# Head 0 of a two-layer graph attention network: raw products first, the logarithm later, some logits earlier

## The chip, the cores and the metric

The kernel runs on one NeuronCore of a Trainium2 chip. The metric is the device time of one execution in microseconds. Three runs of the kernel before are given (median 628.09), and one more execution was profiled. Engines: PE multiplies matrices, DVE and ACT work on vectors, POOL and SP here mainly issue transfers. Each engine works through its own queue in order; engines wait for each other by semaphores.

## The reference

A graph of 512 nodes with 16,896 edges (8,192 random pairs in both directions, and a loop at each node). Node features have 768 columns. Two graph attention layers are followed by a residual and a layer norm; the first layer has 8 heads of 768 columns, the second has one.

```python
h = (x @ W).reshape(n, H, C)
alpha_s = einsum('nhc,hc->nh', h, a_s);  alpha_d = einsum('nhc,hc->nh', h, a_d)
e = leaky_relu(alpha_s[src] + alpha_d[dst], 0.2)
e = exp(e - segment_max(e, dst)[dst])
alpha = e / (segment_sum(e, dst)[dst] + 1e-16)
out = segment_sum(h[src] * alpha[:, :, None], dst) + b
# layer 1 (8 heads, concatenated) -> elu -> layer 2 (1 head)
# result: layernorm(x + layer 2)
```

## The kernel before

Everything is float32. The edges become a dense 512 x 512 matrix of counts `cnt` (how often an edge occurs) and a mask `absent` (a huge number where there is none), in four tiles of 128 target nodes. They are made by products of one-hot matrices while the first projection runs.

Per head of layer 1 there are four stages: the *projection* `HS[h] = x W1[h]`; the *softmax*, for each tile `lift` (ACT), `leak` and `rank` (DVE), an exponential (ACT), `weigh` (DVE), then a transposition by DMA (`turn_out` on ACT and SP, `turn_in` on ACT) into the transposed weights `PT`; the *aggregation* of the features with `PT`, with bias and ELU, into `gT`; and the *second product* `gT W2[h]`, added to `h2`. The softmax of head h+1 runs beside the second product of head h, and its logits (`half_logits`, line 417: a row sum of features times `a_s` or `a_d`, eight for each head, two for each tile) beside the aggregation of head h.

Matrix products use schemes that spare multiplications. The aggregation splits its operands into halves and makes, for each of three chunks `c` of 128 feature columns, seven products P1 to P7 of two matmuls each (each shows as two records) with 256 columns. P1 and P2 multiply raw blocks of the features and of the near half of `PT`. P6, P5, P3 and P4, P7 need sums on one side at least: `left_sums` (lines 932 to 935) of the features, `right_sums` (943 to 946) of `PT`, made by DVE. The results of the seven products are combined by DVE in `u`, `w` and `zr`, and ACT applies the ELU. A product that is added to a bank of another one (P2 to P1, P4 to P7, P3 to P5) has to wait until that bank's first content was read.

The aggregation of heads 0 to 6 is `mixed` (line 949): for each chunk P1, P6, P7, P2, P5, P4, P3. That of head 7 is `last_mixed` (line 1001): the right sums are issued first, then PE does P1 of chunks 0 and 1 and P2 of chunks 0 and 1, and then the other products chunk by chunk. PSUM has five banks named `mm` for all of this, taken in turn.

The second product of head 0 is `by_halves` (line 432): P1, P2, P6, P7, P4, P5, P3, each for two row blocks of three chunk steps. P1 and P2 are emptied by ACT (L445, L446), the others by DVE (L447 to L451). The sums of `gT` are L389 to L392, those of the weights L401 and L402.

In head 0 the softmax multiplies by the counts. From head 1 on the counts are folded into the mask: `logarithm` (line 656) turns `cnt` into its logarithm on ACT, and `fold_count` (line 660) makes `absent - log(cnt)` on DVE. Before the change the logarithm of tile 0 is taken at the end of the projection of head 1, that of tiles 1 to 3 behind the first product of the aggregation of head 0. ACT loads another table for a logarithm (ACT_TABLE_LOAD), and again for the next exponential.

The order of all instructions on each engine is written out by hand; the program is issued in that order (`tc.manual_schedule()`). Near the change: lines 1102 to 1117 issue the second half of head 1's projection with the softmax of head 0 beside it; line 1191 the aggregation of head 0, with lists of what DVE does between its steps; lines 1196 to 1240 the second product of head 0 with the softmax of head 1 beside it. On SP, line 1194 reloads `a_s` and `a_d` for head 2, and `attended` (line 1143) loads four pieces for the second layer, both behind `row_out` (line 622), which sends the source logits of head 1 through DRAM and back as a row.

Of the kernel before, what the change touches and what calls it, by code (L numbers as in the profile page):

```python
# [20 lines left out]
NO_EDGE = -1e30  # L21
# [16 lines left out]
def gat_pass(  # L38
# [515 lines left out]
    def counted(t, ps):  # L554

        nc.scalar.copy(cnt[:, t, :], ps[:, :N])
        nc.scalar.activation(absent[:, t, :], ps[:, :N], AF.Relu, bias=far, scale=NO_EDGE)

    def counted_by_steps(t, ps):


        steps = ohp.tile([P, N + 1], F32, name="steps")
        nc.scalar.activation(steps[:, 1:], ps[:, :N], AF.Copy, scale=0.5)
        nc.scalar.activation(steps[:, :1], ps[:, N - 1:N], AF.Copy, scale=-0.5)
        nc.vector.tensor_tensor(cnt[:, t, :], steps[:, 1:], steps[:, :N], op=ALU.subtract)
        nc.scalar.activation(absent[:, t, :], cnt[:, t, :], AF.Relu, bias=far, scale=NO_EDGE)

    def first_projection(h, XA, B_, between):

# [86 lines left out]
    def logarithm(tiles):  # L656
        nc.scalar.activation(cnt[:, tiles, :], cnt[:, tiles, :], AF.Ln, bias=tiny)
        folded.append(True)
# [19 lines left out]
    if not general:  # L678
# [95 lines left out]
        for n, batch in enumerate(batches):  # L774
            for k in sorted({c // quarter for c in batch} - made):
                destinations(k)
                made.add(k)
            if n + 1 < len(batches):
                sources(kinds(batch, False), waiting)
            if n + 2 == len(batches):  # L780
                sources(kinds(batches[-1], False), [])
            ahead = kinds(batches[n + 1], True) if n + 1 < len(batches) else []
            items_here = max(wants[n] - pos if n < len(wants) else 0, 1)
            share = len(ahead) // (items_here + 1) if n == 0 else -(-len(ahead) // items_here)
            waiting = []
            for f in extra.pop(n, []):
                f()
            while n < len(wants) and pos < wants[n]:
                if pos == wholes:
                    pairs = projection(1, XA, B1)  # L790
                    items += [(m, e, False) for m, e in pairs[:4]]
                multiply, empty, on_vector = items[pos]
                multiply()
                if on_vector:
                    waiting.append(empty)
                else:
                    empty()
                pos += 1
                for t, r in turns.get(pos, []):
                    turn_x(t, r)  # L800
                if pos == 1:
                    nc.scalar.activation(nidx, idx, AF.Copy, bias=0.5, scale=-1.0)
                part = 0 if n == 0 and pos == 2 else share
                for c in ahead[:part]:
                    one_hot(c, True)
                del ahead[:part]
            for c in ahead:
                one_hot(c, True)
            if n == 2:
                turn_b1()  # L810
            if n + 1 == len(batches):
                spread(0)
                q = [lift(0, t) for t in range(NT)]
                for t in range(NT - 1):
                    leak(q[t])
                for t in range(NT - 1):
                    rank(q[t], t)
            if n == 0:
                pst = mm.tile([P, 512], F32, name="mm")
                nc.tensor.matmul(pst[:1, :1], found, ones, start=True, stop=True)  # L820
            if n == 3:
                again = nc.values_load(flag[:1, :1], min_val=0, max_val=E)
            count(batch, n + 1 == len(batches))
# [125 lines left out]
    def mixed(h, A_, B_, fill, ends=()):  # L949

        tt = nc.vector.tensor_tensor
        behind = []

        def some(c, j):
            for f in fill[c][j]:
                f()

        for c in range(HK):
            u = work.tile([P, HN], F32, name="u")
            w = work.tile([P, HN], F32, name="w")  # L960
            zr = work.tile([P, N], F32, name="zr", bufs=3)
            bank = {}

            def part(p, over=None):
                if over is None:
                    bank[p] = mm.tile([P, 512], F32, name="mm")
                else:
                    bank[p] = bank[over]
                for k in range(2):
                    nc.tensor.matmul(bank[p][:, :HN], A_[p][:, k, c * P:(c + 1) * P], B_[p][:, k, :],  # L970
                                     start=over is None and k == 0, stop=k == 1, skip_group_check=True)
                return bank[p][:, :HN]

            nc.scalar.copy(u, part("P1"))  # L974
            if h == c == 0:
                logarithm(slice(1, NT))
            if behind:

                behind = behind[0]()
            tt(u, u, part("P6"), op=ALU.add)  # L980
            tt(w, u, part("P7"), op=ALU.add)
            for f in behind[:1]:
                f()
            near_l = elu(h, c, part("P2", over="P1"), near, "l")
            some(c, 0)
            tt(zr[:, far_], part("P5"), w, op=ALU.subtract)
            for f in behind[1:] + list(ends[:1]) * (c == HK - 1):
                f()
            tt(zr[:, near], u, part("P4", over="P7"), op=ALU.add)
            near_l()  # L990
            for f in list(ends[1:]) * (c == HK - 1):
                f()
            tt(u, part("P3", over="P5"), u, op=ALU.subtract)
            some(c, 1)

            def others(c=c, u=u, zr=zr):
                return [elu(h, HK + c, zr, slice(0, N), "r", spare=zr), elu(h, c, u, far_, "l", spare=u)]
            behind = [others]
        return behind[0]()

    def last_mixed(A_, B_, sums, fill):

        h, tt = H - 1, nc.vector.tensor_tensor
        banks, us, nears = {}, {}, {}

        def part(c, p, over=None):
# [87 lines left out]

    AA, lsums = left_sums(0)
    BB, rsums = right_sums()
    some_logits = half_logits(1, 2)

    def give(t):
        turn_out(q[t], t, weigh(q[t], t, scale=False))  # L1100
# [2 lines left out]
    beside = {4: [lambda: give(0)], 5: [done[4]], 6: [done[5]], 7: [done[6], lambda: give(1)],  # L1103
              8: [done[7], lambda: leak(q[3]), lambda: rank(q[3], 3), lambda: turn_in(0)], 9: [lambda: give(2), done[8]],
              10: [lambda: give(3), lambda: turn_in(1), done[9]], 11: [done[10], lsums[0]],
              12: [done[11], lambda: turn_in(2), *lsums[1:3]], 13: [done[12], lambda: turn_in(3), lambda: logarithm(slice(0, 1)), *rsums[:2]]}
    for n in range(4, 14):
        pairs[n][0]()
        for f in beside[n]:
# [2 lines left out]
            load_w2(0, "w1")()  # L1112
            B2, pending = right(W2[0], "w1")
    pairs[13][1]()
    for f in rsums[2:]:
        f()
    besides = [lsums[3], *some_logits]

    def g_thirds(h):

# [40 lines left out]
    def score(t):  # L1161
        q[t] = lift(h + 1, t)
# [11 lines left out]
    for h in range(H - 1):  # L1174
# [4 lines left out]
        elif h:  # L1179
# [3 lines left out]
                nc.sync.dma_start(v, row_bcast(a))  # L1183
                A[H].append(v)
            last_sum = load_w2(H - 1, "w2")
        halves = [half_logits(h + 1, t) for t in ((0, 1) if h else (0, 1, 3))]
        sources, targets = zip(*halves)
        row = [lambda: row_out(h + 1)]
        if h == 0:
            GA, gsums = left(gT, gS)  # L1190
            finish = mixed(0, AA, BB, [[[besides[0], sources[1]], [besides[1], sources[0]]], [[], [sources[2]] + row + besides[2:]],
                                       [[], list(targets)]])
            load_w1(2)()
            load_a(2, a_src1[2], a_dst1[2])
            attend = attended(0)
# [8 lines left out]
            gsums[1]()  # L1204
            pending[0]()
            pairs[2][0]()
            gsums[2]()
            pairs[3][0]()
            gsums[3]()
            pending[1]()  # L1210
            pairs[2][1]()
            pairs[3][1]()
            fold_count(0)
            score(0)
            for n in range(2, 7):
                (m0, e0), (m1, e1) = pairs[2 * n:2 * n + 2]
                m0()
                m1()
                if n == 3:
                    e0()  # L1220
                if n < 6:
                    scored(n - 2)
                if n < 5:
                    score(n - 1)
                if n == 6:
                    turn_in(0)
                    out_by_dma(2)
                if n != 3:
                    e0()
                if 3 < n < 6:  # L1230
                    out_by_dma(n - 4)
                if n == 6:
                    out_by_dma(3)
                    B2, sums2, load_pairs, load_first, load_rest = load_second(1)
                    load_pairs()
                    load_first()
                    load_rest()
                e1()
                if n < 5:
                    fold_count(n - 1)  # L1240
# [156 lines left out]

    first, second_, third_, fourth = (given(t) for t in range(NT))
    BB, rsums = right_sums()
    finish = last_mixed(AA, BB, [*rsums, lsums[3], lambda: nc.vector.memset(rows, 0.0)], {(1, 1): second_[:1], (2, 1): first})  # L1400
    every = slice(0, N)
    pairs = second(GA, B2)

# [131 lines left out]
```

## Time and profile before

| | |
|---|---|
| runs | 627.80, 628.09, 628.95 us; median 628.09 |
| profiled execution | 628.25 us; its span 626.5 us; granted PE clock 0.997 |
| PE busy | 615.7 us, 98% of the span |
| DVE, ACT, POOL busy | 528.8, 339.2, 148.9 us |
| second half of head 1's projection ends | at 79.0 us |
| aggregation of head 0 | 79.0 to 99.2 us |
| second product of head 0 | 99.2 to 126.4 us |
| aggregation of head 7 | 549.0 to 567.2 us |

In a timeline a row gives start and duration in microseconds, the engine, the line of the kernel, the operation, output and inputs, the shape and how many instructions were merged; in brackets is the engine's idle time before it and what ended it. PEld is the loading of weights into PE, which runs ahead of the matmuls. "q" behind an engine is its queue, which issues transfers. In a list of waits: engine and line, what was waited for, microseconds in total, times, the longest.

### The profile page before, as it was taken

Reading aid. Unit: us, or ns where it says so; the run is one execution under the profiler, and the core shown is the slowest. Engines: PE = TensorE matmul, PEld = TensorE weight load, DVE = VectorE, ACT = ScalarE, POOL = GpSimd, SP = SyncE. Lnnn points to the kernel's source line nnn. Section 1 sums busy time; section 2 is a strip of 40 time slices with the busy share of each in tenths; the row PEclk is TensorE's granted clock in tenths of the full one; section 3 lists DMA queues with packets and bytes.
Section 4 is the critical chain, followed back from the end, with each engine's and each line's share of the span. In section 5 each row is a group of like instructions: output and inputs, shape, how many; then the busy total and the mean of one; then the engine's idle time right before and its main releaser. Section 6 shows DMA issues by size and latency. Waiting matters only on the chain.

```text
span 626.5 us, 8547 instructions
## 1 busy us (share of the span) xinstructions
PE 615.7 (98%) x2765; PEld 483.6 (77%) x2765; DVE 528.8 (84%) x1125; ACT 339.2 (54%) x602; POOL 148.9 (24%) x177
## 2 busy tenths in 40 slices
PE   8999999999999999999999999999999999999995
PEld 5555576556888888888888888888888888886553
DVE  8988979888899879978799778977898778978785
ACT  5874876650658236651658246751658146754361
POOL 1300011013333234323342323323342313010000
PEclk9999999999999999999999999999999999999998
DMA  8994297789999999999999998999999995590042
GB/s 298 326 235 110 67 265 238 188 216 267 249 222 142 326 256 198 172 274 219 248 237 175 308 250 194 194 283 226 228 215 192 317 280 91 107 261 17 17 76 79
DMA packets 109568, 129.45 MB, mean 207 GB/s; under 512 B 41622, under 2 KB 90446, under 8 KB 108750
## 3 DMA queue, kind: packets, MB, share of 16 engines
q1 hardware_dynamic: 75518, 91.35, 47.3%
q0 software_dynamic: 33568, 36.90, 38.4%
q10 hardware_dynamic: 432, 0.59, 0.3%
q8 instruction: 24, 0.39, 0.3%
q14 instruction: 26, 0.21, 0.1%
HBM read 99.84 MB, written 2.90 MB: 164 GB/s over the span
## 4 chain that ended last, share of the span: by engine, by line
PE 86%; ACT 1%; DMA 1%; DVE 1%; issue 0%
PE mm L480 46%; PE mm L970 20%; PE mm L409 13%; PE mm L1481 3%; PE mm L1012 3%; DMA zr<-pS 0%; DMA zr<-nr 0%; ACT PT L907 0%; ACT pS L902 0%; ACT q L899 0%; PE tr L1390 0%; ACT nr L902 0%; PE tr L891 0%; PE bc L1425 0%; DVE hs L1485 0%; PE tr L1427 0%
## 5 line engine op out<-in xcount | busy, mean ns | idle before, releaser
L486 ACT ACTIVATE hs<-mm 128x512 f32<-128x512 f32 x30 | 17.9, 596 | 86.1 <-PE mm L480 85.8
L970 PE MATMUL mm<-PT,hs 128*128 128x256 f32 x252 | 61.3, 379 | 0.0
L970 PEld LDWEIGHTS mm<-PT,hs 128*128 128x128 f32 x252 | 47.8, 190 | 7.3 <-ACT u L974 0.4
L649 ACT ACTIVATE q<-q,nmax 128x512 f32<-128x512 f32 x32 | 23.1, 721 | 51.2 <-DVE nmax L645 50.8
L493 DVE TENSOR_TENSOR hs<-hs,mm 128x512 f32<-128x512 f32 x45 | 30.9, 686 | 22.1 <-PE mm L480 21.3
L491 POOL DMA_DIRECT2D h<-pass x22 | 26.5, 1319 | 80.9 <-ACT pass L490 80.9
L970 PE MATMUL mm<-pS,gS 128*128 128x256 f32 x168 | 43.2, 380 | 1.3 <-DVE pS L944 1.3
L493 DVE TENSOR_TENSOR h<-h,mm 128x512 f32<-128x512 f32 x56 | 38.3, 684 | 6.3 <-PE mm L480 5.8
L907 ACT COPY PT<-zr 128x1024 uint16<-128x1024 uint16 x34 | 39.3, 1155 | 4.2 <-DMA zr<-pS 3.6
L480 PE MATMUL mm<-w2r,xT 128*128 128x256 f32 x160 | 37.8, 379 | 0.0
L480 PE MATMUL mm<-w2r,gT 128*128 128x256 f32 x160 | 37.0, 379 | 0.0
L970 PEld LDWEIGHTS mm<-pS,gS 128*128 128x128 f32 x168 | 31.8, 190 | 5.9 <-DVE pS L944 1.7
L133 POOL DMA_DIRECT2D w1t<-in_L_gnn_W_dram x18 | 29.2, 1642 | 30.4 <-PE mm L409 26.9
L480 PE MATMUL mm<-w1t,hs 128*128 128x256 f32 x144 | 34.1, 380 | 0.0
L480 PE MATMUL mm<-w1r,hs 128*128 128x256 f32 x144 | 34.1, 379 | 0.0
L480 PE MATMUL mm<-w1r,gS 128*128 128x256 f32 x144 | 34.0, 379 | 0.0
L480 PEld LDWEIGHTS mm<-w2r,gT 128*128 128x128 f32 x160 | 30.4, 190 | 4.1
L480 PEld LDWEIGHTS mm<-w2r,xT 128*128 128x128 f32 x160 | 30.4, 190 | 4.1
L974 ACT COPY u<-mm 128x256 f32<-128x256 f32 x21 | 7.8, 371 | 45.5 <-PE mm L970 45.5
L716 DVE TENSOR_SCALAR os<-nodes,idx 128x512 bf16<-128x512 f16 x104 | 29.3, 354 | 1.4 <-PE tr L742 1.4
L480 PEld LDWEIGHTS mm<-w1t,hs 128*128 128x128 f32 x144 | 27.3, 190 | 3.9 <-ACT absent L490 0.2
L480 PEld LDWEIGHTS mm<-w1r,hs 128*128 128x128 f32 x144 | 27.2, 190 | 3.8 <-DVE hs L1130 0.2
(294 smaller groups left out, 1560.8 us busy)
## 6 DMA issues: line engine op xcount, KB each, us to landing
w2r<-in_L_gnn_W_dram SPq DMA_DIRECT2D x48, 384.0 KB
w1r<-in_L_gnn_W_dram SPq DMA_DIRECT2D x43, 384.0 KB
gT<-xd SPq DMA_DIRECT2D x5, 1280.0 KB
w1t<-in_L_gnn_W_dram SPq DMA_DIRECT2D x24, 256.0 KB
h<-pass POOLq DMA_DIRECT2D x22, 256.0 KB, 4.6
w1t<-in_L_gnn_W_dram POOLq DMA_DIRECT2D x18, 256.0 KB, 6.2
w2t<-in_L_gnn_W_dram SPq DMA_DIRECT2D x15, 256.0 KB
w2t<-in_L_gnn_W_dram POOLq DMA_DIRECT2D x15, 256.0 KB, 9.1
```

The source lines that it names most:

```text
L133: nc.gpsimd.dma_start(o, i, accum_op=ALU.add)
L409: nc.tensor.matmul(ps[:, :HALF], A_[p][:, k, i * P:(i + 1) * P], B_[p][:, k, :], start=start and k == 0, stop=k == HK - 1, skip_group_chec ...
L480: nc.tensor.matmul(bank[chain][:, i * TH:(i + 1) * TH], A_[p][:, k, i * P:(i + 1) * P], B_[p][:, k, :], start=first and i == k == 0, stop= ...
L486: nc.scalar.activation(out(o), ps, AF.Copy, scale=sign)
L491: nc.gpsimd.dma_start(out(o), part, accum_op=ALU.add)
L493: nc.vector.tensor_tensor(out(o), out(o), ps, op=ALU.add if sign > 0 else ALU.subtract)
L649: nc.scalar.activation(q, q, AF.Exp, bias=nmax, scale=-1.0, accum_out=dens[t])
L716: nc.vector.tensor_scalar(o, nodes, idx[:, c:c + 1], None, op0=ALU.is_equal)
L907: nc.scalar.copy(PT.rearrange("p s n -> p (s n)").bitcast(U16).rearrange("p (s n h) -> p s n h", s=NT, h=2)[:, :, t * P:(t + 1) * P, :], p ...
L970: nc.tensor.matmul(bank[p][:, :HN], A_[p][:, k, c * P:(c + 1) * P], B_[p][:, k, :], start=over is None and k == 0, stop=k == 1, skip_group ...
L1012: nc.tensor.matmul(banks[c, p][:, :HN], A_[p][:, k, c * P:(c + 1) * P], B_[p][:, k, :], start=over is None and k == 0, stop=k == 1, skip_g ...
L1481: nc.tensor.matmul(ps[:, :cols.stop - cols.start], PT[:, s, t * P:(t + 1) * P], h2[:, s, cols], start=(s == 2), stop=(s == 1))
```

## The change

Four things are done together.

- `last_mixed` becomes `near_first` with the head as an argument, and head 0's aggregation uses it in the place of `mixed`. Its four right sums and the last left sum are issued at its beginning.
- Both logarithms move into the second product of head 0: tile 0 between the two evictions of P2, tiles 1 to 3 behind the lift of tile 0.
- The source logits of tiles 2 and 3 of head 1 move ahead of the right sums, so that the row of head 1 follows the logits of tiles 0 and 1 in chunks 0 and 1. Of the four target logits, those of tiles 2 and 3 stand in chunk 2, those of tiles 0 and 1 in the second product, behind L401 and behind L391.
- In front, `absent` of the count tile that is made by steps (tile 2) is taken on ACT behind two lifts of head 0 instead of ahead of all four.

Instructions of PE, POOL and SP are the same ones; SP's and POOL's order is unchanged.

```diff
+    deferred = []
+
     def counted_by_steps(t, ps):
...
-        nc.scalar.activation(absent[:, t, :], cnt[:, t, :], AF.Relu, bias=far, scale=NO_EDGE)
+        deferred.append(lambda: nc.scalar.activation(absent[:, t, :], cnt[:, t, :], AF.Relu, bias=far, scale=NO_EDGE))
...
-                q = [lift(0, t) for t in range(NT)]
+                q = [lift(0, t) for t in range(2)]
+                for f in deferred:
+                    f()
+                q += [lift(0, t) for t in range(2, NT)]
...
             nc.scalar.copy(u, part("P1"))
-            if h == c == 0:
-                logarithm(slice(1, NT))
...
-    def last_mixed(A_, B_, sums, fill):
-
-        h, tt = H - 1, nc.vector.tensor_tensor
+    def near_first(h, A_, B_, sums, fill):
+
+        tt = nc.vector.tensor_tensor
...
-    some_logits = half_logits(1, 2)
+    some_logits, one_logits = half_logits(1, 2), half_logits(1, 3)
...
-              12: [done[11], lambda: turn_in(2), *lsums[1:3]], 13: [done[12], lambda: turn_in(3), lambda: logarithm(slice(0, 1)), *rsums[:2]]}
+              12: [done[11], lambda: turn_in(2), *lsums[1:3]], 13: [done[12], lambda: turn_in(3), *one_logits[:1], *some_logits[:1]]}
...
     pairs[13][1]()
-    for f in rsums[2:]:
-        f()
-    besides = [lsums[3], *some_logits]
...
-        halves = [half_logits(h + 1, t) for t in ((0, 1) if h else (0, 1, 3))]
+        halves = [half_logits(h + 1, t) for t in (0, 1)]
...
-            finish = mixed(0, AA, BB, [[[besides[0], sources[1]], [besides[1], sources[0]]], [[], [sources[2]] + row + besides[2:]],
-                                       [[], list(targets)]])
+            finish = near_first(0, AA, BB, [*rsums, lsums[3]], {(0, 1): sources[:1], (1, 1): list(sources[1:]) + row, (2, 1): [some_logits[1], one_logits[1]]})
...
             pending[0]()
             pairs[2][0]()
+            targets[0]()
             gsums[2]()
+            targets[1]()
             pairs[3][0]()
             gsums[3]()
             pending[1]()
             pairs[2][1]()
+            logarithm(slice(0, 1))
             pairs[3][1]()
             fold_count(0)
             score(0)
+            logarithm(slice(1, NT))
...
-    finish = last_mixed(AA, BB, [*rsums, lsums[3], lambda: nc.vector.memset(rows, 0.0)], {(1, 1): second_[:1], (2, 1): first})
+    finish = near_first(H - 1, AA, BB, [*rsums, lsums[3], lambda: nc.vector.memset(rows, 0.0)], {(1, 1): second_[:1], (2, 1): first})
```

## The prediction, on record before the result was known

> **What bounds the kernel now.** I read the page first (busy shares, slices, chain), then who waits for whom on PE, then the timeline around the changed lines, and last the same function where the kernel already runs it, in head 7.
>
> ```profile
> span 626.5 us, 8547 instructions
> PE 615.7 (98%) x2765; PEld 483.6 (77%) x2765; DVE 528.8 (84%) x1125; ACT 339.2 (54%) x602; POOL 148.9 (24%) x177
> ...
> PE   8999999999999999999999999999999999999995
> ...
> PE 86%; ACT 1%; DMA 1%; DVE 1%; issue 0%
> ```
>
> PE is busy 98% of the span and carries 86% of the chain that ended last. Its matmuls are the same in both kernels, so a change can win only PE's waits. The longest of these away from the first microseconds:
>
> ```profile
> PE mm L970 <- DVE pS L944: 1.3, 1, 1.3
> ```
> ```profile
> PEld mm L970 <- DVE zr L986: 0.6, 2, 0.4
> ...
> PEld mm L409 <- DVE w1t L401: 0.5, 1, 0.5
> ```
>
> All three lie in head 0, in the aggregation (L970) and the start of the second product (L409), which is what the diff touches. No row of PE or PEld names a DMA. The timeline of that place:
>
> ```profile
> 77.54 0.55 DVE L451 TENSOR_TENSOR hs<-mm,hs 128x384 f32<-128x384 f32 x1
> ...
> 79.00 1.03 PE L970 MATMUL mm<-PT,hs 128*128 128x256 f32 x4
> 79.80 1.28 ACT L657 ACT_TABLE_LOAD   x1
> 79.81 0.69 DVE L943 TENSOR_TENSOR pS<-PT 128x512 f32<-128x512 f32 x1 [1.72 <-ACT PT L907]
> 80.54 0.69 DVE L944 TENSOR_TENSOR pS<-pS,PT 128x512 f32<-128x512 f32 x1
> 81.09 0.72 ACT L657 ACTIVATE cnt<-cnt,tiny 128x512 f32<-128x512 f32 x1
> ...
> 81.28 1.13 PE L970 MATMUL mm<-pS,gS 128*128 128x256 f32 x4 [1.26 <-DVE pS L944]
> ...
> 81.97 1.57 ACT L657 ACTIVATE cnt<-cnt,tiny 128x1536 f32<-128x1536 f32 x1
> ...
> 85.30 1.28 ACT L918 ACT_TABLE_LOAD   x1
> ...
> 86.59 0.42 ACT L918 ACTIVATE nl<-nl 128x256 f32<-128x256 f32 x1
> ...
> 99.19 7.90 PE L409 MATMUL mm<-w1r,gT 128*128 128x384 f32 x24
> ```
>
> The aggregation starts at 79.00, and the second product at 99.19: 20.19 us. After the first product PE stands until L944 has made the sum that P6 multiplies. In front of that sum DVE itself was idle for 1.72 us, waiting for ACT to bring the last quarter of PT.
>
> Head 7 runs the same 21 products in the order that the change gives to head 0:
>
> ```profile
> 549.02 3.62 PE L1012 MATMUL mm<-PT,hs 128*128 128x256 f32 x16
> ...
> 549.90 0.68 DVE L943 TENSOR_TENSOR pS<-PT 128x512 f32<-128x512 f32 x1
> ...
> 552.48 1.03 PE L1012 MATMUL mm<-pS,pass 128*128 128x256 f32 x4
> ...
> 553.49 0.48 DVE L1400 MEMSET tr<- 128x512 f32 x1
> ...
> 553.88 0.41 DVE L1040 TENSOR_TENSOR u<-u,mm 128x256 f32<-128x256 f32 x1
> ...
> 567.20 3.07 PE L409 MATMUL mm<-w2r,gT 128*128 128x384 f32 x9
> ```
>
> From 549.02 to 567.20 is 18.18 us, practically without a wait: four products in 552.48 - 549.02 = 3.46, so 0.865 each, and 21 of them are 18.17. Head 0 therefore loses 20.19 - 18.18 = 2.01 us. That is the most the aggregation can give.
>
> **The change, part by part.** The rows for the DVE queue behind the aggregation, and for what comes after:
>
> ```profile
> 99.39 0.42 DVE L993 TENSOR_TENSOR u<-mm,u 128x256 f32<-128x256 f32 x1
> 99.73 0.95 DVE L418 SCALAR_TENSOR_TENSOR scr<-hs,a_d 128x768 bf16<-128x768 f32 x1
> ...
> 100.73 0.96 DVE L418 SCALAR_TENSOR_TENSOR scr<-hs,a_d 128x768 bf16<-128x768 f32 x1
> ...
> 102.88 0.33 SPq L222 DMA_DIRECT2D a_d<-in_L_gnn_a_dst_dram  x1
> ...
> 105.54 1.35 DVE L401 TENSOR_TENSOR w1t<-w1t,w1r 128x1152 f32<-128x1152 f32 x1
> ...
> 106.94 4.14 PE L409 MATMUL mm<-w1t,gS 128*128 128x384 f32 x12
> ...
> 111.13 0.69 DVE L645 CUSTOM_DVE_ANT_0 q<-q,cnt 128x512 f32<-128x512 f32 x1
> ...
> 111.87 0.72 ACT L649 ACTIVATE q<-q,nmax 128x512 f32<-128x512 f32 x1 [3.64 <-DVE nmax L645]
> ...
> 113.28 0.55 DVE L448 TENSOR_TENSOR h<-h,mm 128x384 f32<-128x384 f32 x1
> ```
> ```profile
> 121.27 0.55 DVE L450 TENSOR_TENSOR h<-mm,h 128x384 f32<-128x384 f32 x1
> ...
> 122.53 4.03 PE L409 MATMUL mm<-w1r,gS 128*128 128x384 f32 x12
> ...
> 126.40 7.90 PE L409 MATMUL mm<-w2r,xT 128*128 128x384 f32 x24
> 127.07 0.95 DVE L1153 SCALAR_TENSOR_TENSOR scr<-w2t,w2t 128x768 bf16<-128x768 f32 x1
> ```
>
> (1) *Raw products first, and two logits ahead of the sums.* Four products that need no sum now cover 4 x 0.865 = 3.46 us, so P6 is wanted at 82.46. DVE: the eviction L451 ends at 78.09; two logits (L418) at 1.00 each, the distance 99.73 to 100.73, fill the 1.72 idle and run to about 80.0; the second L451 (0.55) and the dependent pair L943, L944 (0.73 apart) bring the sum at about 81.85. That is 0.6 before it is wanted. L943 now begins 1.42 after the first product (80.42), in head 7 0.88 after; head 7 has a MEMSET of 0.39 (553.49 to 553.88) in the same list, so DVE stands 0.15 later here at the first u and w, where P4 waits in its turn. I charge 0.15. The second product starts at 79.00 + 18.18 + 0.15 = 97.33: 1.86 earlier. Of the eight logits of head 1 only four are left inside the aggregation.
>
> (2) *The wait for L401.* L993 started 0.20 after the second product, L401 6.15 after L993, with three target logits between. Now there are two: 97.53 + 6.15 - 1.00 = 102.68, end 104.03. P6 of the second product comes four products after its start, at 97.33 + 4 x 1.935 = 105.07 (126.40 - 122.53 = 3.87 for two). No wait there any more.
>
> (3) *What is late next: the DVE queue of the second product.* Two target logits now stand behind L401, 0.9 each without a wait between, 1.8. Before, the first L448 (which frees the bank of P4) ended 113.83 - 105.54 = 8.29 after L401's start: now 102.68 + 8.29 + 1.8 = 112.77, and P4 wants it at 97.33 + 8 x 1.935 = 112.81. It fits by nothing. The first L450 (which frees the bank of P3) ended 16.28 after: now 120.76, wanted at 97.33 + 12 x 1.935 = 120.55. PE waits 0.27, and another 0.1 for the restart, as the four matmuls at 81.28 took 1.13 behind their wait and those at 552.48 1.03: 0.37. The next projection begins at 97.33 + 14 x 1.935 + 0.37 = 124.79, against 126.40: **1.61 us earlier**.
>
> (4) *The logarithm in the second product.* Two Ln (0.72, 1.57) and two table loads (1.28 each) leave the aggregation and come in behind the first P2 eviction: 4.85 us of ACT ahead of Exp L649, which was idle 3.64 before it. P2's first half lands at about 103.3, and its copy ends at 103.8; load, Ln, copy, lift, Ln, load (1.28 + 0.72 + 0.45 + 0.72 + 1.57 + 1.28 = 6.0) end at about 109.8. Exp waits for L645, which ends at 111.82 + 1.8 - 2.86 = 110.76 (L401 starts 2.86 earlier). Cover 1.0 us. Cost nothing; without that cover each microsecond would go to leak and rank, and by them to P3. The fold of tile 0 stands in DVE's queue behind L401 and the two logits, so after 104.03 + 1.8; its Ln is there at 105.8.
>
> (5) *Queues.* The row of head 1 leaves 1.9 earlier, and with it, on SP, the weights of head 2. But the reload of a_d (102.88) waits for the last target logit, now at about 106.7 (L401's end, two logits, a sum between them), and holds four loads of `attended` behind it on SP, 3.8 later. Their reader is L1153, which began at 127.07 with no idle time before it and is now wanted at about 125.5: the loads had 24 us and now have 19. I take nothing, because the row shows no wait; were all 24 us needed, L1153 would be 5 late, which is the upper bound. POOL's order is unchanged.
>
> (6) *Front.*
>
> ```profile
> 59.78 0.72 ACT L566 ACTIVATE absent<-cnt,far 128x512 bf16<-128x512 f32 x1 [1.44 <-DVE cnt L565]
> 60.41 2.40 ACT L636 ACTIVATE q<-tr,al_d 128x512 f32<-128x512 f32 x4
> ...
> 67.29 3.52 PEld L409 LDWEIGHTS mm<-w2t,xT 128*128 128x128 f32 x12 [0.42 <-DVE hs L448]
> ```
>
> Two lifts fill ACT's 1.44, and leak and rank come about 1 us earlier. PE is paced by its own products there; the small wait at 67.29 may go. Bounds 0 and 0.1; I take 0.
>
> The sum is 1.6. The profiled execution took 628.25 (626.5 of it the span), 0.16 above the median 628.09; from 628.25 it becomes 626.65, on the median's scale **626.5 us**. From 126.4 on PE had no wait until the last stage, and transfers start when PE and DVE release their buffers, so they move along.
>
> **The rivals.**
> *A. DVE stays the bound.* Parts 2 and 3 live on margins of 0.0 to 0.3 us, and every tenth that DVE needs more from 78 to 121 goes to PE. If the first L450 does not move at all (121.82), P3 starts at 121.9 + 0.1, and the gain is 122.53 - 122.0 = 0.5: 627.6. For: the logits are only moved, DVE's work is the same. Against: 1.72 us of idle is filled.
> *B. All of it.* If DVE's tail binds nowhere, 2.01 + 0.12 at L401 (106.94 against 99.19 + 4 x 1.935, and a restart of 0.1 counted in) + 0.1 in front: 2.2, so 625.9. Against: the 0.3 of part 3.
> *C. A table switch costs more than its load.* If each of the two held ACT for twice its 1.28, ACT would be ready at 109.8 + 2.56 = 112.4, 1.6 after L645; with up to 0.6 of that taken up where DVE waits for a lift anyway, L450 is 1.0 to 1.6 late: gain 0.0 to 0.6, 627.8. Against: Ln starts at 81.09 after a load from 79.80 to 81.08, and L918 at 86.59 after one from 85.30 to 86.58, at once both times. The Trainium skill, "ScalarE: Activation LUTs", section "What ACT_TABLE_LOAD costs", puts a drain of about 1380 ns beside each load; two of them would be 2.76 us more, an estimate that gives 627.9. The two rows here show no such drain.
> *D. Slower: the softmax of head 1 hangs on ACT.* Exp(0), lift(1), leak, Exp(1) take turns between ACT and DVE, and the evictions L448 to L450 stand behind them in DVE's queue. If ACT's idle time does not cover the 4.85 us, delay beyond 1.0 goes to PE; from 1.0 + 1.6 = 2.6 us the gain is gone, and with all 4.85 it is 1.6 - 3.85 = -2.2: 630.3. Against: 3.64 idle in one piece before L649.
> *E. Given back later.* PE runs 1.6 ahead into weights whose transfers did not move: 628.1. DMA engines are busy nine tenths in most slices, but no PE wait names a DMA.
>
> **How the numbers follow.** Forecast 0.50, A 0.22, B 0.10, C 0.04, D 0.07, E 0.07. 0.2% is 1.26 us, about what a measurement of this kernel tells from no change. The forecast reaches from 626.2 to 627.0, a tenth of it below 1.26 of gain. Faster: 0.45 of the forecast, B, and 0.04 of A: 0.59. Slower: D, and 0.01 of E: 0.08. The rest, 0.33, is the same. The range 625.7 to 628.1 leaves out D, half of E and the rim of B.
>
> **What would show it.** Right: no PE wait for the sum L949 (the old L944); the aggregation some 18.3 long; no PEld wait for w1t; DVE without the gap of 1.72; the second table load over before L647 (the old L645) ends; a wait of PE on L450 below 0.4; the next projection 1.6 earlier and the rest shifted by as much. Wrong: PE waits on L448 or L450 of a microsecond, Exp started by ACT itself rather than by the rank, or new PE waits after 126.

## The result

The kernel after took 626.35 us (median of 6 runs, 625.69 to 626.85), the one before 628.58 on the same chip (6 runs, 627.8 to 628.95): ratio 0.9966 with a 95% interval from 0.9953 to 0.9979, so 2.2 us or 0.35% faster. The profiled execution took 626.73, of which 624.9 is the span.

The page after begins like this (span, busy time of the engines, and the chain that ended last):

```profile
span 624.9 us, 8545 instructions
...
PE 615.7 (99%) x2765; PEld 484.0 (77%) x2765; DVE 528.9 (85%) x1125; ACT 339.4 (54%) x602; POOL 149.0 (24%) x177
...
PE 97%; ACT 2%; DVE 0%; issue 0%; DVEq 0%; ACTq 0%
```

PE's busy time is the same 615.7 as before; only its waits went. Who waits for whom, after, first PE and then its weight loads (total, times, longest):

```profile
PE bc L276 <- DVE zeros L271: 1.3, 1, 1.3
PE mm L409 <- ACT hs L588: 0.3, 1, 0.3
```
```profile
PEld mm L409 <- DVE h L448: 0.7, 2, 0.5
...
PEld mm L409 <- DVE rden L887: 0.5, 1, 0.5
```

The first row belongs to the first microseconds and was there before. The wait of 1.3 for the sum of `PT` and that of 0.5 for `w1t` are gone. New are short ones of the weight loads in the second product: two for L448, 0.7 together, and one of 0.5, which the view puts down to L887 but which ends with L450 (at 121.20). The timeline after, at the place that the prediction showed of before:

```profile
78.38 1.16 ACT L912 COPY PT<-zr 128x1024 uint16<-128x1024 uint16 x1 [0.52 <-DMA zr<-nr]
78.79 0.95 DVE L418 SCALAR_TENSOR_TENSOR scr<-hs,a_s 128x768 bf16<-128x768 f32 x1
...
79.78 3.62 PE L1015 MATMUL mm<-PT,hs 128*128 128x256 f32 x16
81.13 0.68 DVE L948 TENSOR_TENSOR pS<-PT 128x512 f32<-128x512 f32 x1
81.85 0.69 DVE L949 TENSOR_TENSOR pS<-pS,PT 128x512 f32<-128x512 f32 x1
...
83.23 1.03 PE L1015 MATMUL mm<-pS,gS 128*128 128x256 f32 x4
...
97.91 7.90 PE L409 MATMUL mm<-w1r,gT 128*128 128x384 f32 x24
...
104.41 1.28 ACT L659 ACT_TABLE_LOAD   x1
...
105.71 0.72 ACT L659 ACTIVATE cnt<-cnt,tiny 128x512 f32<-128x512 f32 x1
...
108.90 1.28 ACT L651 ACT_TABLE_LOAD   x1
...
110.66 0.69 DVE L647 CUSTOM_DVE_ANT_0 q<-q,cnt 128x512 f32<-128x512 f32 x1
...
111.39 0.72 ACT L651 ACTIVATE q<-q,nmax 128x512 f32<-128x512 f32 x1 [1.21 <-DVE nmax L647]
112.81 0.55 DVE L448 TENSOR_TENSOR h<-h,mm 128x384 f32<-128x384 f32 x1
...
113.41 1.59 PEld L409 LDWEIGHTS mm<-w1t,gT 128*128 128x128 f32 x6 [0.48 <-DVE h L448]
...
120.65 0.55 DVE L450 TENSOR_TENSOR h<-mm,h 128x384 f32<-128x384 f32 x1
...
121.26 4.14 PE L409 MATMUL mm<-w1r,gS 128*128 128x384 f32 x12
...
125.23 5.00 PE L409 MATMUL mm<-w2r,xT 128*128 128x384 f32 x15
```

PE now runs four products (3.62) while DVE makes the sum, which is ready at 82.54 and wanted at 83.23, and DVE has no idle time noted in front of L948 (1.72 before). From the aggregation's start to the next projection it is 125.23 - 79.78 = 45.45, against 126.40 - 79.00 = 47.40: **1.95 us less**. Of this, the aggregation gives 2.06 (18.13 against 20.19), and the second product takes back 0.11 (27.32 against 27.21). The same two stages in the view by windows (window, length, PE, PEld, DVE, ACT, POOL busy, clock, DMA share, GB/s), first before, then after:

```profile
79.00:99.19 20.19, 18.90 (x85) 15.71 (x84) 16.92 (x38) 16.22 (x30) 2.56 (x2) 1.00 0.76 211
99.19:126.40 27.21, 27.21 (x86) 15.88 (x85) 23.53 (x49) 16.17 (x29) 2.53 (x2) 1.00 0.86 248
```
```profile
79.78:97.91 18.13, 18.13 (x85) 15.84 (x84) 15.18 (x34) 10.79 (x25) 2.56 (x2) 1.00 0.80 223
97.91:125.23 27.32, 27.32 (x85) 15.79 (x84) 24.27 (x51) 20.13 (x32) 2.53 (x2) 1.00 0.84 244
```

By this view PE is busy from end to end of both stages (a product counts up to its modelled end, so delays of 0.1 do not show in it); ACT has 5.4 us less work in the first and 4.0 more in the second, DVE 1.7 less and 0.7 more. Between the aggregations of heads 1 and 7 both kernels take the same time (395.53 before, 395.54 after). The spans differ by 1.6 only, because the profiled execution after was 0.85 later at its first products already: one and the same product of head 1's projection starts at 59.47 before and at 60.33 after. That differs from run to run; over all the kernels below it starts between 59.23 and 60.52, and at 60.52 in logs_only, which is the kernel before up to there. Apart from it and the 1.95, a wait of 0.08 went ahead of the aggregation (below), and the stretch from the start of head 7's aggregation to the end is 0.37 shorter, which also scatters: over all the kernels below it lies between 77.06 and 77.48.

### The profile page after: what moved, and what is told of

It is laid out like the page before. It is cut to its first block, busy times and chain, and to the rows that moved or that the text cites. A ratio compares the mean times of both kernels' runs of the same rounds, so it can differ in the third digit from the quotient of the medians.

```text
span 624.9 us, 8545 instructions
## 1 busy us (share of the span) xinstructions
PE 615.7 (99%) x2765; PEld 484.0 (77%) x2765; DVE 528.9 (85%) x1125; ACT 339.4 (54%) x602; POOL 149.0 (24%) x177
## 4 chain that ended last, share of the span: by engine, by line
PE 97%; ACT 2%; DVE 0%; issue 0%; DVEq 0%; ACTq 0%
PE mm L480 46%; PE mm L409 19%; PE mm L975 17%; PE mm L1015 6%; PE mm L1484 3%; PE held L409 2%; ACT os L716 1%; PE tr L744 1%; PE held L610 1%; PE bc L276 1%; PE mm L307 0%; PE bc L744 0%; PE tr L1393 0%; ACT xT L308 0%; PE tr L896 0%
## 5 line engine op out<-in xcount | busy, mean ns | idle before, releaser
L975 PE MATMUL mm<-PT,hs 128*128 128x256 f32 x216 | 52.5, 379 | 0.0
L975 PEld LDWEIGHTS mm<-PT,hs 128*128 128x128 f32 x216 | 41.0, 190 | 5.8
L975 PE MATMUL mm<-pS,gS 128*128 128x256 f32 x144 | 37.0, 379 | 0.0
L975 PEld LDWEIGHTS mm<-pS,gS 128*128 128x128 f32 x144 | 27.4, 190 | 3.7
L480 PEld LDWEIGHTS mm<-w1r,gS 128*128 128x128 f32 x144 | 27.3, 190 | 3.7
```

What stands on the lines that cost most here:

```text
L480: nc.tensor.matmul(bank[chain][:, i * TH:(i + 1) * TH], A_[p][:, k, i * P:(i + 1) * P], B_[p][:, k, :], start=first and i == k == 0, stop= ...
```

## The experiments

The theory: head 0's aggregation was bound by the late sum of `PT`, the new order hides it, and what is then late next is DVE's tail in the second product, which fits by almost nothing. Against it stood: the order alone would do (or the logarithm alone); ACT, not DVE, carries the second product; the table loads cost more than they show. The table gives for each kernel the ratio to the kernel before on the same chip, and from its trace the two stages and their sum. For order_only, two_more, switch_2 and fold_pool the stages are the safer measure, since their medians hold executions with a lower granted clock (last section).

| kernel | median us | ratio [95%] | aggregation, head 0 | second product | sum |
|---|---|---|---|---|---|
| before | 628.58 | 1 | 20.19 | 27.21 | 47.40 |
| after | 626.35 | 0.9966 [0.9953, 0.9979] | 18.13 | 27.32 | 45.45 |
| logs_only | 628.16 | 0.9995 [0.9985, 1.0005] | 20.20 | 27.20 | 47.41 |
| order_only | 630.66 | 1.0033 [1.0023, 1.0043] | 21.78 | 27.20 | 48.98 |
| logs_back | 628.04 | 0.9989 [0.9980, 0.9999] | 19.48 | 27.32 | 46.80 |
| order_back | 628.85 | 1.0007 [0.9997, 1.0016] | 20.18 | 27.32 | 47.51 |
| logits_back | 627.28 | 0.9977 [0.9966, 0.9987] | 19.13 | 27.31 | 46.44 |
| targets_back | 627.31 | 0.9980 [0.9970, 0.9989] | 18.13 | 28.20 | 46.33 |
| front_back | 626.32 | 0.9972 [0.9962, 0.9983] | 18.13 | 27.32 | 45.45 |
| two_more | 628.61 | 1.0012 [1.0001, 1.0023] | 18.13 | 29.32 | 47.45 |
| switch_1 | 628.36 | 0.9999 [0.9989, 1.0008] | 18.13 | 28.83 | 46.96 |
| switch_2 | 632.47 | 1.0057 [1.0040, 1.0074] | 18.13 | 31.95 | 50.08 |
| fold_pool | 630.57 | 1.0038 [1.0024, 1.0052] | 18.13 | 30.18 | 48.31 |

### One part alone: the logarithm, the order

From the kernel before, only the logarithm moved into the second product:

```diff
-13: [done[12], lambda: turn_in(3), lambda: logarithm(slice(0, 1)), *rsums[:2]]
+13: [done[12], lambda: turn_in(3), *rsums[:2]]
...
-            if h == c == 0:
-                logarithm(slice(1, NT))
...
             pairs[2][1]()
+            logarithm(slice(0, 1))
             pairs[3][1]()
             fold_count(0)
             score(0)
+            logarithm(slice(1, NT))
```

> The kernel before with both logarithms moved into the second product and nothing else. Measured is the stretch from the first product of head 0's aggregation to the first product of head 2's projection: 47.40 us before, 45.45 after. My theory (the sum behind the last quarter of PT sets the first wait, and ACT is not in its way): 47.2 to 47.4, so no change of the time beyond 0.2 us; the aggregation stays at 20.0 to 20.2. Rival, each of the parts brings its own share of the 2 us: some 46.9 or less. Rival C, a table switch holds ACT beyond the row of its load: slower in the second product, 48 or more.

It changed nothing: 20.20 and 27.20. The sum that PE waits for does not hang on the logarithm in the old order, and ACT has room for it in either place.

From the kernel before, only the order of head 0's products, with the logarithm and the logits where they were (`near_first` is `last_mixed` with the head as an argument, and takes the logarithm of tiles 1 to 3 behind its first copy, as `mixed` did):

```diff
-            finish = mixed(0, AA, BB, [[[besides[0], sources[1]], [besides[1], sources[0]]], [[], [sources[2]] + row + besides[2:]],
-                                       [[], list(targets)]])
+            finish = near_first(0, AA, BB, besides[:1], {(0, 0): [sources[1]], (0, 1): [besides[1], sources[0]],
+                                (1, 1): [sources[2]] + row + besides[2:], (2, 1): list(targets)})
```

> The kernel before with head 0 aggregated by the function of head 7, the logarithms left in the aggregation and the logits behind the sums. My theory: worse than before, because P2 of chunks 0 and 1 now stands early in PE's queue and waits for the copies of P1 on ACT, which stand behind a table load and two logarithms: waits of about 1.2 and 0.8 us at P2, another 0.9 at P3 and P4; the stretch 48.4 to 48.8, so 1.0 to 1.4 us slower than before. Rival, each part brings its own share: the raw products first save the 1.4 us wait for the sum, 46.0.

It is slower by 1.58 in the aggregation, a little more than expected, and by 0.33% in all. The view of waits shows why:

```profile
PE mm L1012 <- ACT u L1018: 1.8, 2, 1.2
...
PE mm L1012 <- DVE w L1045: 0.7, 1, 0.7
```

P2 adds to the bank of P1 and has to wait until ACT has copied P1 into `u`. In the new order P2 is the third product, and the copy stands on ACT behind a table load and the logarithm. In the old order P2 was the fourth product of its chunk, and the same delay of ACT cost nothing (logs_only). The wait for `w` is that of P4 in chunk 1, which logits_back below shows by itself.

### One part taken back from the whole

The logarithm put back in front, everything else as after:

```diff
-13: [done[12], lambda: turn_in(3), *one_logits[:1], *some_logits[:1]]
+13: [done[12], lambda: turn_in(3), lambda: logarithm(slice(0, 1)), *one_logits[:1], *some_logits[:1]]
...
             nc.scalar.copy(us[c], part(c, "P1"))
+            if h == c == 0:
+                logarithm(slice(1, NT))
...
-            logarithm(slice(0, 1))
             pairs[3][1]()
...
-            logarithm(slice(1, NT))
```

> The changed kernel with the logarithms back in the aggregation (tile 0 ahead of the first P1 copy, tiles 1 to 3 behind it). My theory: PE waits at P2 of chunk 0 for 1.2 and at P2 of chunk 1 for 0.8 us; the aggregation 20.2 to 20.5, the stretch 47.4 to 47.9, so the whole gain of the change is gone (about 2.1 us slower than the changed kernel). Rival, parts add up: the logarithm's move is worth no more than 0.3 us, stretch 45.8.

The place is as expected, the size was not: the two waits are 0.37 and 0.77 with 0.1 of restart each, so 1.35 in all. (They are counted from when the product would have followed at 0.865 each; the brackets below, 0.21 and 0.61, count from the modelled end of the product before.)

```profile
77.48 1.16 ACT L912 COPY PT<-zr 128x1024 uint16<-128x1024 uint16 x1 [0.49 <-DMA zr<-nr]
78.66 1.28 ACT L659 ACT_TABLE_LOAD   x1
78.89 1.89 PE L1015 MATMUL mm<-PT,hs 128*128 128x256 f32 x8
79.96 0.72 ACT L659 ACTIVATE cnt<-cnt,tiny 128x512 f32<-128x512 f32 x1
80.59 0.35 ACT L1021 COPY u<-mm 128x256 f32<-128x256 f32 x1
80.84 1.57 ACT L659 ACTIVATE cnt<-cnt,tiny 128x1536 f32<-128x1536 f32 x1
80.99 1.13 PE L1015 MATMUL mm<-PT,hs 128*128 128x256 f32 x4 [0.21 <-ACT u L1021]
82.32 0.36 ACT L1021 COPY u<-mm 128x256 f32<-128x256 f32 x1
...
82.73 1.13 PE L1015 MATMUL mm<-PT,hs 128*128 128x256 f32 x4 [0.61 <-ACT u L1021]
```

The last quarter of `PT` is copied here 1.41 ahead of the first product (77.48 against 78.89), in the kernel before 0.38 ahead (78.62 against 79.00), so the table load starts 0.23 before the first product and not 0.80 after it. That 1.03 is what the moved `absent` in front brings: leak and rank of head 0 run about 1 us earlier, as step 6 said: in front_back, without that move, the copy is 0.35 ahead again (79.00 against 79.35). I had left it out of the expectation.

The order put back, everything else as after:

```diff
-            finish = near_first(0, AA, BB, [*rsums, lsums[3]], {(0, 1): sources[:1], (1, 1): list(sources[1:]) + row,
-                                (2, 1): [some_logits[1], one_logits[1]]})
+            for f in rsums:
+                f()
+            finish = mixed(0, AA, BB, [[[lsums[3]], [sources[0]]], [[], list(sources[1:]) + row], [[], [some_logits[1], one_logits[1]]]])
```

> The changed kernel with head 0 aggregated chunk by chunk as before, P6 as the second product; the logarithms in the second product and the two logits ahead of the sums stay. My theory: with the logits ahead the sum of PT comes at 2.8 us after the first product instead of 2.2, P6 waits 2.0 for it, and more is lost at P4 to P3 of chunk 0: aggregation 21.2 to 22.0, stretch 48.5 to 49.4, slower than the kernel before by 1 to 2 us. Rival, the raw products bring only the 1.4 us wait: stretch 46.9.

```profile
PE mm L975 <- DVE pS L949: 1.8, 1, 1.8
```

The second product of the chunk waits 1.8 for the sum, since the two logits in front of it now delay it, and the whole gain is gone (47.51). The further loss that I expected in chunk 0 did not come. From after, then, the order is worth 2.06, and the logarithm's place 1.35; alone they were worth -1.58 and 0.00.

Two logits back to their old place behind the sums:

```diff
-13: [done[12], lambda: turn_in(3), *one_logits[:1], *some_logits[:1]]
+13: [done[12], lambda: turn_in(3)]
...
-{(0, 1): sources[:1], (1, 1): list(sources[1:]) + row, (2, 1): [some_logits[1], one_logits[1]]}
+{(0, 1): [sources[0], one_logits[0]], (1, 1): [sources[1], some_logits[0]] + row, (2, 1): [some_logits[1], one_logits[1]]}
```

> The changed kernel with the two source logits back behind the sums (in chunks 0 and 1). DVE then waits again 1.7 us for the last quarter of PT. My theory: the sum still comes in time, the products of chunk 1 wait for DVE by about 0.75 us and the tail in the second product stays bound by DVE: stretch 46.1 to 46.5, 0.7 to 1.0 slower than the changed kernel. Rival B (DVE binds nowhere): 45.4 to 45.5, no difference. Rival A (DVE binds throughout): the full 1.7 us, 47.1.

```profile
90.88 1.13 PE L1015 MATMUL mm<-pS,hs 128*128 128x256 f32 x4 [0.66 <-DVE w L1046]
```

0.99 lost, as expected: two logits in a row now stand in front of `u` and `w` of chunk 1, and P4 of that chunk, which adds to the bank that `w` reads, starts 0.82 later than it would have followed. Filling DVE's idle time ahead of the sums is thus worth half of the gain, though the sums themselves are in time without it.

The two target logits put back from the second product into the aggregation:

```diff
-                                (2, 1): [some_logits[1], one_logits[1]]})
+                                (2, 1): [some_logits[1], one_logits[1], *targets]})
...
-            targets[0]()
             gsums[2]()
-            targets[1]()
```

> The changed kernel with all four target logits in chunk 2 of the aggregation, none behind L401. My theory: the sum of the weights comes 1.9 us later and PE waits for it at P6 by about 0.7 us, with a restart of 0.1; the DVE tail behind it is as late as in the changed kernel, so its two small waits go: stretch 45.9 to 46.4, 0.5 to 0.9 slower than the changed kernel. Rival, the targets could stand anywhere on DVE: 45.4.

```profile
106.68 4.14 PE L409 MATMUL mm<-w1t,gS 128*128 128x384 f32 x12 [0.74 <-DVE w1t L401]
```

0.88 lost, as expected, at the wait for L401 that the kernel before had too: step 2.

The edit in front undone (`absent` computed at once and not deferred):

```diff
-        deferred.append(lambda: nc.scalar.activation(absent[:, t, :], cnt[:, t, :], AF.Relu, bias=far, scale=NO_EDGE))
+        nc.scalar.activation(absent[:, t, :], cnt[:, t, :], AF.Relu, bias=far, scale=NO_EDGE)
```

> The changed kernel with the mask of tile 2 taken ahead of all four lifts, as before. My theory: the small wait of P4 of head 1's projection for L448 comes back, 0.08 us; the time the same within 0.1. Rival: the whole softmax of head 0 comes 1 us later and delays the aggregation: 0.5 us or more.

The wait of the weight loads for L448 is back (0.43 at 67.64), the stretch from P6 of head 1's projection to the aggregation is 19.53 as before, not 19.45, and the time is that of after.

### What bounds the second product

Two target logits computed twice, so that DVE has about 1.9 us more ahead of its tail:

```diff
             targets[1]()
+            targets[0]()
+            targets[1]()
```

> The changed kernel with the two target logits behind L391 computed a second time (1.8 us more on DVE, the same values). It measures how far the DVE queue of the second product is the bound. My theory (margins of 0.0 to 0.3 at L448 and L450): almost all of it reaches PE, mostly as one wait of P4 for the first L448: stretch 46.9 to 47.4, 1.5 to 1.9 slower. Rival B (DVE binds nowhere, there is cover): under 45.9.

```profile
PE mm L409 <- DVE h L448: 1.9, 1, 1.9
```

All of it reached PE: the second product is 2.00 longer, and the time is back at that of before. DVE's tail really has no room.

One or two needless changes of ACT's table between the two logarithms, about 3.0 us of ACT each (two loads of 1.28, two functions of 0.20 and 0.29 on one column):

```diff
             score(0)
+            idle_col = small.tile([P, 1], F32, name="idle_col", bufs=1)
+            for _ in range(1):
+                nc.scalar.activation(idle_col, ones, AF.Exp)
+                nc.scalar.activation(idle_col, ones, AF.Ln, bias=tiny)
             logarithm(slice(1, NT))
```

switch_2 is the same with `range(2)`.

> The changed kernel with one exponential and one logarithm of a 128x1 tile between the lift of tile 0 and the logarithm of tiles 1 to 3: two more table loads, about 2.9 us more on ACT. The second load ended 1.2 us before the rank of tile 0 in the changed kernel, so 1.7 us reach the softmax. My theory: part of it is taken up by DVE's work ahead of leak, PE loses 0.5 to 1.2 us: stretch 46.0 to 46.7. Rival C (a switch costs more than its load, 2.66 each): 4.0 us or more between the two loads and their functions, the stretch over 47.5.

> The same with two rounds, four more table loads, about 5.8 us more on ACT. My theory (rival D's mechanism, priced): beyond the cover of ACT every microsecond reaches PE: 2.7 to 3.2 us more than with one round, stretch 48.8 to 49.8, so slower than the kernel before. Rival, the softmax has more slack than that: 47.5 or less.

```profile
107.18 1.28 ACT L1219 ACT_TABLE_LOAD   x1
108.47 0.20 ACT L1219 ACTIVATE idle_col<-ones 128x1 f32<-128x1 f32 x1
108.69 1.28 ACT L1220 ACT_TABLE_LOAD   x1
109.99 0.29 ACT L1220 ACTIVATE idle_col<-ones,tiny 128x1 f32<-128x1 f32 x1
110.19 1.56 ACT L659 ACTIVATE cnt<-cnt,tiny 128x1536 f32<-128x1536 f32 x1
111.77 1.28 ACT L651 ACT_TABLE_LOAD   x1
113.06 0.72 ACT L651 ACTIVATE q<-q,nmax 128x512 f32<-128x512 f32 x1
```

These rows are of switch_1. The exponential no longer waits for the rank but for its own load, and begins 15.40 after the start of the second product instead of 13.48 (113.06 - 97.66, 111.39 - 97.91): 1.92 later. The long logarithm starts 3.12 later (110.19 - 97.66, 107.32 - 97.91), and ACT had idled 1.21, so this is to be expected. Of the 1.92, 1.51 reached PE, more than I expected (0.5 to 1.2), mainly as one wait:

```profile
PE mm L409 <- DVE h L448: 1.1, 1, 1.1
```

The second needless change cost 3.12, all of it. So ACT has 1.2 us of room; what is beyond reached PE by four fifths in the first change and whole in the second. Both kernels lost more elsewhere in the profiled execution, 1.6 and 2.15 between the aggregations of heads 1 and 7; see the last section.

To give DVE the room that it lacks, the fold was moved to POOL:

```diff
     def fold_count(t):
 
-        nc.vector.tensor_tensor(cnt[:, t, :], absent[:, t, :], cnt[:, t, :], op=ALU.subtract)
+        nc.gpsimd.tensor_tensor(cnt[:, t, :], absent[:, t, :], cnt[:, t, :], op=ALU.subtract)
```

> The changed kernel with the four folds of the counts on POOL instead of DVE: 2.4 us less in the DVE queue of the second product. My theory: the two remaining waits of PE (P4 for L448, P3 for L450, 0.23 us together) go: stretch 45.2, 0.2 us less, not to be told from no change in the whole time. Rival: POOL's fold comes too late for the rank, and PE waits more: 45.6 or more.

It missed: the two stages are 2.86 longer than after, and 0.91 longer than before.

```profile
105.42 1.78 POOL L664 TENSOR_TENSOR cnt<-absent,cnt 128x512 f32<-128x512 bf16 x1
...
106.11 1.91 DVE L392 TENSOR_TENSOR gS<-gT,gS 128x768 f32<-128x768 f32 x1
...
107.86 4.98 POOL L664 TENSOR_TENSOR cnt<-absent,cnt 128x512 f32<-128x512 bf16 x3 [0.66 <-ACT cnt L659]
107.95 2.31 DVE L402 TENSOR_TENSOR w1t<-w1t,w1r 128x1152 f32<-128x1152 f32 x1
110.18 1.65 DVE L642 SCALAR_TENSOR_TENSOR q<-q 128x512 f32<-128x512 f32 x1
111.97 1.42 DVE L647 CUSTOM_DVE_ANT_0 q<-q,cnt 128x512 f32<-128x512 f32 x1
...
114.86 4.30 PE L409 MATMUL mm<-w1t,gT 128*128 128x384 f32 x12 [2.40 <-DVE h L448]
```

While POOL folds, four of DVE's instructions take up to 2.4 times their time: a sum of 768 columns 1.91, where the one before it (L391, without a fold beside it) took 0.95; L402 2.31 against 1.35 in after; L642 1.65 and L647 1.42, each 0.69 once POOL is done. Together this is 3.6 more, and the four folds of 0.68 that DVE was spared are 2.7.

## Why the prediction was right

It said 626.5 from a gain of 1.6; measured were 626.35 and a gain of 2.2 by the medians. By stages the gain is 1.95 and the 0.08 in front, 2.03. That the time came out nearer than the gain is luck: the forecast set out from the median of three runs (628.09), six runs gave 628.58, and these 0.49 hide most of the 0.6 by which the gain was too small.

1. *Raw products first.* Right in place, 0.20 too small. It gave 2.06 instead of 1.86. The 0.15 charged for DVE standing later at the first `u` and `w` was not there: the second product starts 18.13 after the aggregation, `w` of chunk 0 is ready at 85.61 and P4, which waits for it, starts at 85.82 without a wait, while P4 of head 7, the measure, has a wait of 0.18 of its weight loads for `w`. Its bound of 2.01 was short by 0.05: head 7, its measure, takes 18.18, that much more than head 0 does now.
2. *The wait for L401.* Right; targets_back brings it back and costs 0.88.
3. *DVE's tail.* Right in mechanism, 0.27 too dear in its P3 term, with a small one missing. (The wait of 0.27 inside that term is 0.21 by the two times that it names, 120.76 and 120.55.) L448 was forecast to end 15.44 after the start of the second product (112.77 - 97.33) and ended 15.45 after it (113.36 - 97.91): "it fits by nothing" held, and it cost PE 0.13, which the sum did not have (the second product is 0.23 longer than its 14 x 1.935, and 0.10 of it is P3's). L450 was forecast to end 23.43 after it and ended 23.29 after it, so that P3 lost 0.10 instead of 0.37. The kernel before had lost 0.12 at L401, so the second product is 0.11 longer. two_more shows that the tail does bind: 2.0 more on DVE are 2.0 more in time.
4. *The logarithm in the second product.* Right. The second load is over at 110.18, the exponential waits until 111.39 for the rank: 1.21 of cover, where 1.0 was worked out. switch_1 and switch_2 show the price once it is gone; there PE first met the delay at L448, ahead of P4's second half, and not at P3 as the step had it. What the step did not say is that this edit pays nothing by itself (logs_only); it is what keeps the new order from waiting on ACT (order_only, logs_back).
5. *Queues.* Right. The reload of `a_d` and the four loads behind it left later, and their reader L1153 began 0.68 after the next projection, as before (125.91 and 125.23; 127.07 and 126.40), with no idle time ahead of it.
6. *Front.* 0.08 of the bound 0.1, taken as 0. That `PT` is complete 1 us earlier was foreseen as an effect and not as a gain: with everything in place it brings none (front_back), but it softened logs_back.

The rivals: *A* (DVE stays the bound) had the right place, but there was just room enough. *B* (2.2, nothing binds) came closer in size than the forecast, but DVE's tail does bind: the two tenths that are missing from it are those at P4 and P3. *C* is refuted: in after, the first logarithm starts 0.02 after the end of its load (104.41 + 1.28 = 105.69, and 105.71), and in switch_1 the row of loads and functions from 107.18 to 113.06 leaves no gap above 0.02. The drain of about 1380 ns that the Trainium skill, "ScalarE: Activation LUTs", section "What ACT_TABLE_LOAD costs", puts beside a load shows in none of them; there the measurement decides. *D* is a real mechanism with a threshold of 1.2 us that this change stays under. *E* (given back later) did not happen: 395.53 and 395.54 between the aggregations of heads 1 and 7.

## What to carry to other kernels

Parts of a reordering are not terms of a sum: here the logarithm alone was worth nothing and the order alone cost 1.6, and all four parts together gave 2. Taken out of the whole one at a time, the order, the logarithm, the two source logits and the two target logits cost 2.06, 1.35, 0.99 and 0.88, together far more than the gain, since the new order only pays once the instruction that it now depends on early (ACT's copy of P1) stands behind nothing. So look, for each product that moves forward, at what is queued ahead of the engine that frees its bank. And follow the queue of the next engine to the end of the stage: a forecast of when each eviction ends, by distances taken from the old trace, was good to 0.15 us over 23 us.

## What was not expected of the hardware

*Folding on POOL slows DVE.* One fold of 128x512 took 0.68 on DVE; on POOL four took 1178 to 2274 ns with a median of 1691, and the DVE instructions beside them stretched as shown. The Trainium skill, "SBUF — State Buffer", section "SBUF: two separate sides", says that DVE with two inputs in SBUF and a GpSimd operation that reads SBUF exclude each other for a whole instruction. The trace agrees, turn by turn: the folds (the merged row of three taken apart) end at 107.20, 109.04, 111.28 and 112.85, each 1.02 to 1.03 behind the end of the DVE instruction that was running when it started (L418, L392, L402, L642, at 106.18, 108.02, 110.26 and 111.83), and L392, L402, L642 and L647 end 0.82, 1.23, 0.54 and 0.54 behind a fold, 0.13 to 0.15 less than they take alone. That this lock is the cause was not tested by itself.

*A later wait in four kernels.* In the profiled executions of order_only and order_back, the stretch between the aggregations of heads 1 and 7 took 0.35 longer than in after, in switch_1 1.6 and in switch_2 2.15. The latter two show it as one wait each, in different places:

```profile
PE mm L480 <- DVE hs L493: 1.4, 1, 1.4
```
```profile
PE mm L480 <- DMA gT<-xd: 1.9, 1, 1.9
```

All four are kernels in which head 0 ends late, but in their profiled executions two_more and fold_pool end late too and do not have it. switch_1's median is about that of before, although its trace, with this wait, is 1.5 longer in its span, so the wait is hardly in every run. Its cause stays open.

*A lower granted clock in some executions.* In 13 executions of four kernels (3 of 10 in order_only, 4 of 10 in two_more, 2 of 4 in switch_2, 4 of 5 in fold_pool) the granted clock is 0.992 to 0.995; in all others of this document, the kernel before included, it is 0.996 or more. In two_more those took 629.97 to 630.46 us, the other six 628.24 to 628.62; in fold_pool 630.35 to 630.85, and the profiled one, at 0.997, 628.55 (in order_only the difference is about 1.5, in switch_2 it is not clear). The 2 us are about what the clock makes: 0.35% of PE's 616 us busy is 2.2, an estimate. In all four kernels PE waits once for 1.2 us or more in head 0, but so it does in before (1.3) and order_back (1.8), where no such execution was seen. No profile was taken of one, so the cause stays open.
